# A two-layer graph network on one core: the first 32 tiles of layer one are taken from the edge list as it comes

## The chip, the core and the metric

The kernel runs on one core of one Trainium2 chip. The metric is the device time of one execution in microseconds (us), lower is better. The core has a matrix engine (PE, whose weight loads are listed as PEld), a vector engine (DVE), an activation engine (ACT), a general engine (POOL, also called GpSimd), which here issues the indirect DMAs, and a sync engine (SP), which issues most other DMAs. All DMAs run on 16 shared DMA engines.

## The reference

There are 12,500 nodes with 64 features and 212,500 edges: 200,000 drawn ones and one loop per node. The edges are sorted by target `dst`, and the loop of a node comes last among its edges.

```
h = max(layernorm(x), 0)
x = x + L0(h, weight, src, dst, etypes)
h = max(layernorm(x), 0)
x = x + L1(h, (src, dst), edge_attr, W1, b1, W2, b2)

L0: for r in range(16):
        msg += (feat[src] * (etypes == r)) @ weight[r]
    out = segment_sum(msg, dst)
L1: h = relu(concat(x[src], x[dst], edge_attr) @ W1 + b1)
    out = segment_sum(h @ W2 + b2, dst)
```

## The kernel before

**Tiles and groups.** Edges are worked off in tiles of 128, and tiles in groups of G = 4. Layer one leaves the loops out of its tiles (their part is put into the sums by `begin` and `some`, lines 724 to 763), so the edge list is first closed up: `compact` (line 427) takes one of eight parts of rows, moves the remaining edges together on DVE, and `store` (line 474) writes them to `edges_c` in memory by two indirect DMAs on POOL. `load_tiles` (line 547) loads them back as tiles (`t_in`, `t_row`), and `codes` (line 558) works out for each tile the source indices `src_c`, a code per edge (relation and place within the tile's window of WT = 12 targets) and the window's place in the running table. This makes 1563 closed-up tiles in 391 groups. The list UPTO says which tiles belong to which part; part 0 has 188.

**The front.** `load_front` (line 250) loads all of x by SP, `front` (line 265) normalizes it in nine chunks on DVE and ACT, and SP stores each chunk to `h_rows` in memory. `compact` and `codes` of part 0 run between the chunks. The first gather of layer one reads `h_rows`, so it comes after the last store. POOL meanwhile does memsets and iotas and loads the weights (lines 349 to 377: `none`, `wrel` twice, `first_row`, `place_row`, `w1ab` twice, `b1_bc`, `w2b` twice, `zero`), eleven DMAs.

**Layer one** is the loop at lines 867 to 919. In turn `it` it gathers group `it`: `gather` (line 618) issues four indirect DMAs on POOL, each of which brings 128 rows of 256 bytes into a `rows` buffer; there are 14 of these (pool `land`). `relations` (line 631) makes one-hot rows `oh_r` of relation and place on ACT, four `Abs` (`off_r`) and one `Relu` per group, with four buffers. `products` (line 845) multiplies on PE, and `add` (line 855) adds the product to the table on DVE at a place read from a row of places. The first products wait for turn BEGIN + 1 = 9, and the adds for turn 10, since the table has to be begun by then, which needs the loops of the first nodes (`loops`, line 490, on DVE, stored to `t_loop` by POOL in turns 3 and 4). From there two groups are worked off per turn until the lag is gone; `turns` (line 106) makes these orders. Each of the 47 long steps FIN1 ends a pair of node blocks: `finish` (line 657) multiplies the table by `wrel` (`pT`), adds to x, normalizes, and stores `a_rows` and `b_rows`.

**Work beside it.** `beside_part(c)` (line 816) is a generator that is advanced by one step with each add. It prepares part c + 1 (`load_rows`, `compact`, `load_tiles`, `codes`), loads further loops and so on. What is left of it is done where the next part begins.

**Layer two** (line 947) gathers `a_rows` in 416 groups in the same manner. SP loads a window of `b_rows` for each group into one of NBW = 10 buffers `b_win`.

**Order.** Instructions issued through the wrappers `V_, S_, T_, Q_, P_` (class `InOrder`, lines 301 to 315) keep the order of the program on DVE, ACT, PE, SP and POOL; all others are placed by a scheduler that knows only estimated durations. Most of layers one and two goes through the wrappers, and the profile gives these instructions the wrapper's line, L310. Each engine runs its queue in order and waits at an instruction whose data is not there.

**Bounds.** Where the fixed windows of a program step hold the edges is decided by the data, so `bounds` (line 133) lists limits on `dst` at some edges; if one fails, `flag` is set and a general program, `in_any_order`, runs behind.

The order of the start is this:

```
h_of = front(fr, xf)
for _ in range(2):
    next(h_of)
for _ in compact(0, rows_0, V, lambda n: ()):
    pass
q, row = load_tiles(0, nc.sync)
for _ in range(3):
    next(h_of)
for _ in codes(0, q, row, psA, V, S, T, lambda n: ()):
    pass
loops_0 = load_loops(0)
```

Of the kernel before, what the change touches and what calls it, by code (L numbers as in the profile page):

```python
# [45 lines left out]
P = 128  # L48
# [35 lines left out]
CL = 202  # L84
PARTS = EP // (P * ROW)
UPTO = [0, 188, 384, 580, 776, 972, 1168, 1364, 2 * -(-NTC // 2)]
PMAX = max(b - a for a, b in zip(UPTO, UPTO[1:]))
# [17 lines left out]

def turns(lag, n, early=lambda g: 0):

    most, least = lag
    of = {}
    for g in range(n):  # L110
        of.setdefault(max(early(g), g + max(least, min(most, most - (g - (n - 40)) // 4))), []).append(g)
    return of
# [15 lines left out]

FIN1 = [8 * (k + 1) + SLACK - 1 for k in range(NREG)] + [384, 388, NGC - 1]
STEP1 = [sum(f < g for f in FIN1) for g in range(NGC)]  # L130


def bounds():

    least, most = [(0, 0)], [(0, 0)]
    for k in range(NFIN - 1):
        b0, nb = BLOCKS[k]
        end = (b0 + nb) * P

        x = (FIN1[k] + 1) * G * P  # L140
        least.append((x + end, end))
        ahead = end + AHEAD - WT
        if x + ahead < E:
            most.append((x + ahead, ahead))
        x = (FIN[k] + 1) * G * P
        least.append((x, end))
        most.append((min(x, E) - 1, end + AHEAD2 - W))
    for c in range(1, PARTS):
        most.append((c * P * ROW, c * P * ROW - UPTO[c] * P))
    for q in range(1, LPARTS):  # L150
        least.append((q * P * LROW, LOOPS_UPTO[q]))
    return least, most
# [3 lines left out]
WE = W + EA  # L156
NBW = 10
RG = 8
# [21 lines left out]
def gnn_kernel(  # L180
    ctx: ExitStack, tc, x, src, dst, etype, attr, src_t, dst_t, attr_t, rows_c, rows_l, first, last, step_t, step_c, least, most, w_rel, w1, b1, w2, b2, out
):
# [33 lines left out]

    NCK = 3 * PARTS + 4 * LPARTS + 3
    odds = keep.tile([P, NCK], F32, name="odds")
# [66 lines left out]
    def in_order():  # L285
        with ExitStack() as c2:
# [42 lines left out]
            c4 = c3.enter_context(ExitStack())  # L329
            fr = c4.enter_context(tc.tile_pool(name="front", bufs=2))  # L330
            rows_0 = load_rows(0, nc.sync)
            xf = load_front(fr)
# [15 lines left out]
            G_.memset(none, -1.0)  # L348
            G_.dma_start(t_loop[N:, :].rearrange("n o -> o n"), none)
            wrel = own.tile([P, RH, D], F32, name="wrel")  # L350
            for k in range(2):
                G_.dma_start(wrel[k * D : (k + 1) * D], w_rel[k::2].rearrange("r i o -> i r o"))
# [3 lines left out]
            G_.dma_start(first_row, first.unsqueeze(0))  # L356
# [3 lines left out]
            G_.dma_start(place_row, step_t[::G].unsqueeze(0))  # L360
            w1ab = own.tile([P, 2, D], F32, name="w1ab")
            for k in range(2):
                G_.dma_start(w1ab[k * D : (k + 1) * D], w1[: 2 * D].rearrange("(k i) o -> i k o", k=2))
            b1_bc = own.tile([P, D], F32, name="b1_bc")
            G_.dma_start(b1_bc, b1.unsqueeze(0).to_broadcast([P, D]))
            w2b = own.tile([DA, D], F32, name="w2b")
            G_.dma_start(w2b[:D, :], w2)
            G_.dma_start(w2b[D:DA, :], b2.unsqueeze(0))

# [6 lines left out]
            G_.memset(zero, 0.0)  # L376
            G_.dma_start(b_rows[NB * P :, :], zero)

# [95 lines left out]
            def store(table, to, rows, rest, pause=16):  # L474

                for half in range(2):
# [6 lines left out]
                    yield from rest(pause)  # L483

            def load_loops(q):
# [72 lines left out]
            def codes(c, q, row, psA, V, S, T, rest):  # L558
# [9 lines left out]
                codes_of[c] = code, places  # L568
                word, first_d = q[:n, :, :, 0], q[:n, :, 0, 1]
                low, rel, even = (i_[:n, k] for k in range(3))  # L570
                sf, d, ok = (f[:n, k] for k in range(3))
# [225 lines left out]
            def chain(*parts):  # L797
                for part in parts:
                    yield from part
# [27 lines left out]

            def first_layer(psA, loops_0):
# [6 lines left out]
                n_of, oh_of, rows_of, pa_of = {}, {}, {}, {}  # L835
                of_pe = turns(L1_PE, NGC, lambda g: BEGIN + 1 + g // 2)
                of_add = turns(L1_ADD, NGC, lambda g: BEGIN + 2 + g // 2)
                of_oh = turns((0, 0), NGC, lambda g: BEGIN + g // 2 if g < 2 * BEGIN else 0)

                def part_of(g):  # L840

                    c = sum(g * G >= b for b in UPTO[1:])
                    return c, g * G - UPTO[c]

# [10 lines left out]
                def add(a, i):  # L855
                    k = a * G + i
                    if i < n_of[a]:
                        ca, ka = part_of(a)
                        ka += i
                        if ka % RG == 0:  # L860
                            n = min(RG, UPTO[ca + 1] - UPTO[ca] - ka)
                            at.update(enumerate(windows(codes_of[ca][1], ka, SN + AHEAD - WT, V_, n), k))
                        to = tables[STEP1[a] % 2][:, :, bass.ds(at.pop(k), WT)]
                        V_.tensor_tensor(to, to, pa_of[a][:, i, :].rearrange("p (r n) -> p r n", r=RH), op=ALU.add)

                at = {}
                for it in range(NGC + L1_ADD[1]):
                    g = it
                    if g < NGC:
                        c, kc = part_of(g)  # L870
                        if kc == 0:
# [3 lines left out]
                        if g % 56 == 16 and g // 56 < NB // LB:  # L875
                            load_x(g // 56 * LB, Q_)
                        rows_of[g], n_of[g] = gather(h_rows[:, :], src_c, g, NTC)
                    for g in of_oh.get(it, []):
                        c, kc = part_of(g)
                        oh_of[g] = relations(codes_of[c][0], kc, n_of[g])  # L880
                    if it < BEGIN:
                        for _ in range(G):
                            next(first_loops, None)
                        if it == BEGIN - 2:
                            for _ in first_loops:
                                pass
# [628 lines left out]
```

## Time and profile before

| what | us |
|---|---|
| median of 3 runs (lowest to highest) | 4140.85 (4140.67 to 4142.58) |
| the profiled execution | 4139.85 |
| its span in the profile | 4137.5 |
| POOL busy | 3083.6 |
| PE busy / weight loads | 2619.0 / 2087.4 |
| ACT busy | 1609.3 |
| DVE busy | 1136.7 |
| first gather of `h_rows` starts | 50.19 |
| POOL waits between the layers, once | 17.2 |

Spans and medians are of single executions; busy times are sums over one engine's instructions. A line of a timeline gives the start, the duration, the engine, the line, the operation, output and input, the count, and in brackets how long the engine was idle before and what ended it. An engine name with a q (SPq) is the queue that issues DMAs; its time is that of issuing, not of the transfer. In a row of windows each engine has its busy time and its number of instructions; then come the clock granted to PE (1.00 is full), the busy share of the 16 DMA engines and the GB/s moved.

PE's granted clock is 1.00 for the first 75 us and 0.50 from 125 us on.

### The profile page before, as it was taken

Reading aid. Unit: us, or ns where it says so; the run is one execution under the profiler, and the core shown is the slowest. Engines: PE = TensorE matmul, PEld = TensorE weight load, DVE = VectorE, ACT = ScalarE, POOL = GpSimd, SP = SyncE. Lnnn points to the kernel's source line nnn. Section 1 sums busy time; section 2 is a strip of 40 time slices with the busy share of each in tenths; the row PEclk is TensorE's granted clock in tenths of the full one; section 3 lists DMA queues with packets and bytes.
Section 4 is the critical chain, followed back from the end, with each engine's and each line's share of the span. In section 5 each row is a group of like instructions: output and inputs, shape, how many; then the busy total and the mean of one; then the engine's idle time right before and its main releaser. Section 6 shows DMA issues by size and latency. Waiting matters only on the chain. (4 is left out here: it accounts for less than half of the span.)

```text
span 4137.5 us, 50346 instructions
## 1 busy us (share of the span) xinstructions
PE 2619.0 (63%) x15332; PEld 2087.4 (50%) x15332; DVE 1136.7 (27%) x4570; ACT 1609.3 (39%) x3131; POOL 3083.6 (75%) x3279
## 2 busy tenths in 40 slices
PE   1676666667676767666666666665666666666655
PEld 0444444444444444444555555555555555555555
DVE  6343334333343333323211111111111111111111
ACT  5545454444444444544422322322322223223222
POOL 5777777777777777777677777777777777777776
PEclk9555555555555555555555555555555555555555
DMA  4212222112212121111111211212121221112111
GB/s 111 47 38 53 47 43 49 41 37 44 43 42 45 37 45 38 38 38 37 39 42 40 44 41 40 45 40 44 41 42 42 43 42 42 42 41 44 42 39 34
DMA packets 217607, 180.05 MB, mean 44 GB/s; under 512 B 147587, under 2 KB 156198, under 8 KB 216390
## 3 DMA queue, kind: packets, MB, share of 16 engines
q0 software_dynamic: 104576, 107.96, 14.2%
q1 hardware_dynamic: 99453, 65.57, 5.9%
q10 hardware_dynamic: 13298, 3.20, 0.3%
q8 instruction: 125, 2.05, 0.2%
q14 instruction: 155, 1.27, 0.1%
HBM read 161.49 MB, written 14.99 MB: 43 GB/s over the span
## 5 line engine op out<-in xcount | busy, mean ns | idle before, releaser
L310 POOL DMA_INDIRECT rows<-a_rows,src_i x1661 | 1567.1, 943 | 523.3 <-issue 426.2
L310 POOL DMA_INDIRECT rows<-h_rows,src_c x1563 | 1483.4, 949 | 503.7 <-issue 390.7
L310 PE MATMUL pz<-b_win,of_edges 48*128 48x64 f32 x3322 | 815.4, 424 | 712.7 <-ACT of_edges L310 708.4
L310 PE MATMUL pa<-oh_r,rows 128*64 128x96 f32 x6252 | 856.9, 387 | 621.4 <-DMA rows<-h_rows,src_c 552.3
L310 PEld LDWEIGHTS pz<-b_win,of_edges 48*128 48x128 f32 x3322 | 738.5, 325 | 760.8 <-ACT of_edges L310 739.7
L310 PEld LDWEIGHTS pa<-oh_r,rows 128*64 128x64 f32 x6252 | 471.1, 207 | 941.1 <-DMA rows<-h_rows,src_c 615.9
L310 ACT ACTIVATE hid<-z 128x256 f32<-128x256 f32 x416 | 173.1, 416 | 1449.7 <-DVE z L310 1399.2
L310 DVE TENSOR_TENSOR z<-pz,rows 128x256 f32<-128x256 f32 x416 | 176.5, 424 | 1692.9 <-DMA rows<-a_rows,src_i 1539.9
L310 ACT ACTIVATE off_r<-iota_s,code 128x192 bf16<-128x192 f32 x1563 | 578.6, 442 | 1.9 <-issue 1.9
L310 PE MATMUL pa<-oh,hid 128*65 128x40 f32 x3322 | 456.7, 312 | 39.8 <-ACT hid L310 26.9
L310 DVE TENSOR_TENSOR table<-table,pa 128x96 f32 x1563 | 395.5, 253 | 301.6 <-PE pa L310 194.3
L310 ACT ACTIVATE oh_r<-off_r 128x768 f32<-128x768 bf16 x391 | 329.3, 842 | 302.2 <-PE pa L310 292.6
L310 PEld LDWEIGHTS pa<-oh,hid 128*65 128x65 f32 x3322 | 395.9, 226 | 90.0 <-ACT hid L310 30.9
L310 PE MATMUL pT<-wrel,table 128*128 128x64 f32 x1568 | 432.5, 434 | 0.0
L310 PEld LDWEIGHTS pT<-wrel,table 128*128 128x128 f32 x1568 | 362.8, 324 | 82.8 <-issue 82.5
L310 ACT ACTIVATE off<-local_bc,neg_w 40x1024 bf16<-40x1024 bf16 x208 | 235.8, 1134 | 15.6 <-DVE sums L310 8.3
L310 ACT ACTIVATE of_edges<-off 40x1024 f32<-40x1024 bf16 x208 | 219.7, 1056 | 6.6
L310 DVE SCALAR_TENSOR_TENSOR table<-b_rel,rsel,hT 128x256 f32<-128x256 f32 (+1 forms) x400 | 172.4, 472 | 96.3 <-PE hT L310 73.0
L310 DVE TENSOR_TENSOR ab<-pab,b_bc 128x64 f32<-128x64 f32 x98 | 17.6, 220 | 432.3 <-ACT ab L310 432.3
L310 DVE TENSOR_TENSOR oh<-local,iota_p 128x160 f32<-128x160 f32 x416 | 128.8, 310 | 0.0
L310 DVE TENSOR_TENSOR x_sb<-x_sb,pT 128x128 f32<-128x128 f32 (+1 forms) x50 | 14.2, 285 | 397.3 <-PE pT L310 397.3
L310 ACT ACTIVATE s_rs<-s_mv,eps 128x2 f32<-128x2 f32 (+1 forms) x50 | 14.8, 296 | 242.2 <-DVE s_mv L310 238.0
(163 smaller groups left out, 840.7 us busy)
## 6 DMA issues: line engine op xcount, KB each, us to landing
rows<-a_rows,src_i POOLq DMA_INDIRECT x1661, 2.5
rows<-h_rows,src_c POOLq DMA_INDIRECT x1563, 2.4
local_bc<-dst_l SPq DMA_DIRECT2D x104, 160.0 KB
of_edges<-in_attr_t SPq DMA_DIRECT2D x104, 64.0 KB
b_win<-b_rows SPq DMA_DIRECT2D x416, 10.0 KB
b_rel<-t_loop SPq DMA_DIRECT2D x48, 128.0 KB
l_in<-in_rows_l SPq DMA_DIRECT2D x4, 1009.5 KB
b_h<-h_rows SPq DMA_DIRECT2D x48, 64.0 KB
```

The source lines that it names most:

```text
L310: last_ins[self.engine] = getattr(self.engine, name)(*args, **kw)
```

## The change

The first eight groups of layer one (RAWG = 8, 32 tiles, 4096 edges) are taken from the edge list as it stands, with the loops in it, and the first 28 closed-up tiles (CUT = 28) are left out. For the 32 raw tiles POOL gathers rows of `x` itself, not of `h_rows`, while the front runs; the gathered rows are normalized afterwards, in place (`rows_raw`). Loops and edges of no relation get a code that matches nothing (`codes_raw`). Closed-up tiles 28 to 30 or so hold edges that are among the 4096 too; `codes` of part 0 masks those by their place in the list (`place_w`). 

The group numbers of layer one shift by SHIFT = 8 - 28/4 = 1, so there are 392 groups, of which 384 are gathered within the loop, and the loop's turn `it` gathers group it + 8. At turn BEGIN = 8, when products begin, 16 groups are waiting where 8 were.

The eleven weight DMAs move from POOL's start into a generator `weights` on SP's ordered queue, as the first steps of `beside_part(0)`. The number of `b_win` buffers goes from 10 to 8. Two limits on `dst` are added to the bounds.

```
+RAWG = 8
+RAWT = RAWG * G
+RAWE = RAWT * P
+CUT = 28
+SHIFT = RAWG - CUT // G
+NG1 = NGC + SHIFT
...
+    most.append((RAWE, RAWE - CUT * P))
+    most.append((RAWE - 1, SN + AHEAD - WT))
...
-NBW = 10
+NBW = 8
...
+            raw = own.tile([P, 4, RAWT], I32, name="raw")
+            nc.sync.dma_start(raw, raw_c)
+            raw_rows = [own.tile([P, 2, G, D], F32, name=f"raw_rows{k}") for k in range(RAWG // 2)]
+            raw_tiles = iter(range(RAWT))
+            def gather_raw(n):
+                for _, k in zip(range(n), raw_tiles):
+                    g, i = divmod(k, G)
+                    P_.indirect_dma_start(
+                        out=raw_rows[g // 2][:, g % 2, i, :],
+                        out_offset=None,
+                        in_=x[:, :],
+                        in_offset=bass.IndirectOffsetOnAxis(ap=raw[:, 3, k : k + 1], axis=0),
+                    )
+                return ()
             rows_0 = load_rows(0, nc.sync)
...
-            G_.dma_start(t_loop[N:, :].rearrange("n o -> o n"), none)
...
+            def weights():
+                for k in range(2):
+                    Q_.dma_start(wrel[k * D : (k + 1) * D], w_rel[k::2].rearrange("r i o -> i r o"))
+                    Q_.dma_start(w1ab[k * D : (k + 1) * D], w1[: 2 * D].rearrange("(k i) o -> i k o", k=2))
+                    yield
...
+            def codes_raw():
...
+                Q_.dma_start(f, raw_f.unsqueeze(0).to_broadcast([P, RAWT]))
+                Q_.dma_start(row, raw_f.unsqueeze(0))
...
+            def rows_raw(k):
+                n = 2 * G
+                r = raw_rows[k].rearrange("p a g d -> p (a g) d")
...
+                for i in range(n):
+                    V_.bn_stats(st[:, i, :], r[:, i, :])
+                for i in range(n):
+                    V_.bn_aggr(mv[:, i, :], st[:, i, :])
+                S_.activation(rs[:, 0, :], mv[:, :, 1], AF.Sqrt, bias=eps, scale=1.0)
+                yield
+                V_.reciprocal(rs[:, 1, :], rs[:, 0, :])
+                V_.scalar_tensor_tensor(rs[:, 2, :], mv[:, :, 0], -1.0, rs[:, 1, :], op0=ALU.mult, op1=ALU.mult)
+                for i in range(n):
+                    S_.activation(r[:, i, :], r[:, i, :], AF.Relu, bias=rs[:, 2, i : i + 1], scale=rs[:, 1, i : i + 1])
+                yield
...
+                if c == 0:
+                    place_w = prep.tile([PMAX // 2, 2, P], F32, name="t_place", bufs=1)[:n]
+                    G_.iota(place_w, pattern=[[P, 2], [1, P]], base=0, channel_multiplier=2 * P, allow_small_or_imprecise_dtypes=True)
+                    V.tensor_tensor(place_w, place_w, q[:n, :, :, 1], op=ALU.add)
...
+                if c == 0:
+                    V.scalar_tensor_tensor(ok, place_w, float(RAWE), ok, op0=ALU.is_ge, op1=ALU.mult)
...
             def beside_part(c, psA):
+                if c == 0:
+                    yield from weights()
...
+                more = chain(codes_raw(), *(rows_raw(k) for k in range(RAWG // 2)))
...
-                for it in range(NGC + L1_ADD[1]):
-                    g = it
-                    if g < NGC:
+                for it in range(NG1 - RAWG + L1_ADD[1]):
+                    g = it + RAWG
+                    if g < NG1:
...
                     if it < BEGIN:
                         for _ in range(G):
                             next(first_loops, None)
+                        for _ in range(2):
+                            next(more, None)
...
-                for _ in compact(0, rows_0, V, lambda n: ()):
+                gather_raw(9)
+                for _ in compact(0, rows_0, V, lambda n: gather_raw(4) if n > 8 else ()):
                     pass
+                gather_raw(RAWT)
                 q, row = load_tiles(0, nc.sync)
```

The raw gathers go through the ordered wrapper of POOL: nine, then compact's first store, four, its second store, four, and the remaining fifteen.

More of the change, by code (lines that the diff above doesn't have):

```diff
@@ L103, with turns @@
 BEGIN = 8
-def turns(lag, n, early=lambda g: 0):
+def turns(lag, n, early=lambda g: 0, before=0):
     most, least = lag
@@ L110, in turns @@
     for g in range(n):
-        of.setdefault(max(early(g), g + max(least, min(most, most - (g - (n - 40)) // 4))), []).append(g)
+        of.setdefault(max(early(g), g - before + max(least, min(most, most - (g - (n - 40)) // 4))), []).append(g)
     return of
@@ L127 @@
 STEP = [sum(f < g for f in FIN) for g in range(NGR)]
-FIN1 = [8 * (k + 1) + SLACK - 1 for k in range(NREG)] + [384, 388, NGC - 1]
-STEP1 = [sum(f < g for f in FIN1) for g in range(NGC)]
+FIN1 = [8 * (k + 1) + SLACK - 1 + SHIFT for k in range(NREG)] + [384 + SHIFT, 388 + SHIFT, NG1 - 1]
+STEP1 = [sum(f < g for f in FIN1) for g in range(NG1)]
 def bounds():
@@ L138, in bounds @@
         end = (b0 + nb) * P
-        x = (FIN1[k] + 1) * G * P
+        x = (FIN1[k] + 1 - SHIFT) * G * P
         least.append((x + end, end))
@@ L180, in gnn_kernel @@
 def gnn_kernel(
-    ctx: ExitStack, tc, x, src, dst, etype, attr, src_t, dst_t, attr_t, rows_c, rows_l, first, last, step_t, step_c, least, most, w_rel, w1, b1, w2, b2, out
+    ctx: ExitStack, tc, x, src, dst, etype, attr, src_t, dst_t, attr_t, rows_c, rows_l, raw_c, raw_f, first, last, step_t, step_c, least, most, w_rel, w1, b1, w2, b2, out
 ):
@@ L215, in gnn_kernel @@
     flag = keep.tile([1, 1], I32, name="flag")
-    NCK = 3 * PARTS + 4 * LPARTS + 3
+    NCK = 3 * PARTS + 4 * LPARTS + 4
     odds = keep.tile([P, NCK], F32, name="odds")
@@ L348, in in_order @@
             G_.memset(none, -1.0)
-            G_.dma_start(t_loop[N:, :].rearrange("n o -> o n"), none)
             wrel = own.tile([P, RH, D], F32, name="wrel")
-            for k in range(2):
-                G_.dma_start(wrel[k * D : (k + 1) * D], w_rel[k::2].rearrange("r i o -> i r o"))
             local = own.tile([P, NT], F32, name="local")
@@ L355, in in_order @@
             first_row = own.tile([1, NGR], I32, name="first_row")
-            G_.dma_start(first_row, first.unsqueeze(0))
             src_i = own.tile([P, NT], I32, name="src_i")
             place_row = own.tile([1, NGR], I32, name="place_row")
-            G_.dma_start(place_row, step_t[::G].unsqueeze(0))
             w1ab = own.tile([P, 2, D], F32, name="w1ab")
-            for k in range(2):
-                G_.dma_start(w1ab[k * D : (k + 1) * D], w1[: 2 * D].rearrange("(k i) o -> i k o", k=2))
             b1_bc = own.tile([P, D], F32, name="b1_bc")
-            G_.dma_start(b1_bc, b1.unsqueeze(0).to_broadcast([P, D]))
             w2b = own.tile([DA, D], F32, name="w2b")
-            G_.dma_start(w2b[:D, :], w2)
-            G_.dma_start(w2b[D:DA, :], b2.unsqueeze(0))
             b_win = [own.tile([WE, D], F32, name=f"b_win{k}") for k in range(NBW)]
@@ L376, in in_order @@
             G_.memset(zero, 0.0)
-            G_.dma_start(b_rows[NB * P :, :], zero)
+            def weights():
[3 more added lines that the diff above has]
+                    yield
+                Q_.dma_start(b1_bc, b1.unsqueeze(0).to_broadcast([P, D]))
+                Q_.dma_start(t_loop[N:, :].rearrange("n o -> o n"), none)
+                yield
+                Q_.dma_start(first_row, first.unsqueeze(0))
+                Q_.dma_start(place_row, step_t[::G].unsqueeze(0))
+                yield
+                Q_.dma_start(w2b[:D, :], w2)
+                Q_.dma_start(w2b[D:DA, :], b2.unsqueeze(0))
+                yield
+                Q_.dma_start(b_rows[NB * P :, :], zero)
+                yield
             def rest(n):
@@ L483, in store @@
                     yield from rest(pause)
+            raw_code = own.tile([P, RAWT], F32, name="raw_code")
+            raw_places = own.tile([1, RAWT], I32, name="raw_places")
+            def codes_raw():
+                f = prep.tile([P, RAWT], I32, name="raw_f", bufs=1)
+                row = prep.tile([1, RAWT], I32, name="raw_r", bufs=1)
+                even = prep.tile([P, RAWT], I32, name="raw_e", bufs=1)
+                rel = prep.tile([P, RAWT], I32, name="raw_t", bufs=1)
+                d = prep.tile([P, RAWT], F32, name="raw_d", bufs=1)
+                ok = prep.tile([P, RAWT], F32, name="raw_ok", bufs=1)
+                bad = prep.tile([P, RAWT], F32, name="raw_bad", bufs=1)
+                Q_.dma_start(f, raw_f.unsqueeze(0).to_broadcast([P, RAWT]))
+                Q_.dma_start(row, raw_f.unsqueeze(0))
+                dst_r, next_r, typ_r = raw[:, 0], raw[:, 1], raw[:, 2]
+                V_.tensor_scalar(rel, typ_r, 1.0, 0.0, op0=ALU.add, op1=ALU.max)
+                V_.tensor_single_scalar(rel, rel, float(R + 1), op=ALU.min)
+                V_.tensor_single_scalar(even, rel, 1, op=ALU.bitwise_and)
+                yield
+                V_.tensor_tensor(ok, dst_r, next_r, op=ALU.is_equal)
+                V_.scalar_tensor_tensor(ok, rel, 1.0, ok, op0=ALU.is_ge, op1=ALU.mult)
+                V_.scalar_tensor_tensor(ok, rel, float(R), ok, op0=ALU.is_le, op1=ALU.mult)
+                yield
+                V_.tensor_tensor(d, dst_r, f, op=ALU.subtract)
+                V_.scalar_tensor_tensor(bad, d, float(WT), d, op0=ALU.is_ge, op1=ALU.mult, accum_out=next(odds_of))
+                V_.scalar_tensor_tensor(d, rel, float(WT // 2), d, op0=ALU.mult, op1=ALU.add)
+                yield
+                V_.scalar_tensor_tensor(d, even, -float(HW - WT // 2), d, op0=ALU.mult, op1=ALU.add)
+                V_.scalar_tensor_tensor(d, d, float(1 + HW - WT), ok, op0=ALU.add, op1=ALU.mult)
+                V_.tensor_scalar(raw_code, d, -1.0, 1.0, op0=ALU.mult, op1=ALU.add)
+                yield
+                V_.tensor_scalar(raw_places, row, 0.0, float(SN + AHEAD - WT), op0=ALU.max, op1=ALU.min)
+                yield
@@ new lines, in rows_raw @@
+            def rows_raw(k):
+                n = 2 * G
+                r = raw_rows[k].rearrange("p a g d -> p (a g) d")
+                st = prep.tile([P, n, 6], F32, name="raw_st")
+                mv = prep.tile([P, n, 2], F32, name="raw_mv")
+                rs = prep.tile([P, 3, n], F32, name="raw_rs")
+                for i in range(n):
[3 more added lines that the diff above has]
+                S_.activation(rs[:, 0, :], mv[:, :, 1], AF.Sqrt, bias=eps, scale=1.0)
+                yield
+                V_.reciprocal(rs[:, 1, :], rs[:, 0, :])
+                V_.scalar_tensor_tensor(rs[:, 2, :], mv[:, :, 0], -1.0, rs[:, 1, :], op0=ALU.mult, op1=ALU.mult)
+                for i in range(n):
+                    S_.activation(r[:, i, :], r[:, i, :], AF.Relu, bias=rs[:, 2, i : i + 1], scale=rs[:, 1, i : i + 1])
+                yield
@@ L835, in first_layer @@
                 n_of, oh_of, rows_of, pa_of = {}, {}, {}, {}
-                of_pe = turns(L1_PE, NGC, lambda g: BEGIN + 1 + g // 2)
-                of_add = turns(L1_ADD, NGC, lambda g: BEGIN + 2 + g // 2)
-                of_oh = turns((0, 0), NGC, lambda g: BEGIN + g // 2 if g < 2 * BEGIN else 0)
-                def part_of(g):
-                    c = sum(g * G >= b for b in UPTO[1:])
-                    return c, g * G - UPTO[c]
+                of_pe = turns(L1_PE, NG1, lambda g: BEGIN + 1 + g // 2, RAWG)
+                of_add = turns(L1_ADD, NG1, lambda g: BEGIN + 2 + g // 2, RAWG)
+                of_oh = turns((0, 0), NG1, lambda g: BEGIN + g // 2, RAWG)
+                for g in range(RAWG):
+                    rows_of[g], n_of[g] = raw_rows[g // 2][:, g % 2], G
+                more = chain(codes_raw(), *(rows_raw(k) for k in range(RAWG // 2)))
+                def part_of(g):
+                    if g < RAWG:
+                        return (raw_code, raw_places), g * G, RAWT
+                    k = (g - SHIFT) * G
+                    c = sum(k >= b for b in UPTO[1:])
+                    return codes_of[c], k - UPTO[c], UPTO[c + 1] - UPTO[c]
                 def products(g, i):
@@ L857, in add @@
                     if i < n_of[a]:
-                        ca, ka = part_of(a)
+                        of, ka, n = part_of(a)
                         ka += i
-                        if ka % RG == 0:
-                            n = min(RG, UPTO[ca + 1] - UPTO[ca] - ka)
-                            at.update(enumerate(windows(codes_of[ca][1], ka, SN + AHEAD - WT, V_, n), k))
+                        if k not in at:
+                            n = min(RG - ka % RG, n - ka)
+                            at.update(enumerate(windows(of[1], ka, SN + AHEAD - WT, V_, n), k))
                         to = tables[STEP1[a] % 2][:, :, bass.ds(at.pop(k), WT)]
@@ L866, in first_layer @@
                 at = {}
-                for it in range(NGC + L1_ADD[1]):
-                    g = it
-                    if g < NGC:
-                        c, kc = part_of(g)
-                        if kc == 0:
+                for it in range(NG1 - RAWG + L1_ADD[1]):
+                    g = it + RAWG
+                    if g < NG1:
+                        k = (g - SHIFT) * G
+                        if it == 0 or k in UPTO:
+                            c = sum(k >= b for b in UPTO[1:])
                             for _ in coming:
@@ L874, in first_layer @@
                             coming = beside_part(c, psA)
-                        if g % 56 == 16 and g // 56 < NB // LB:
-                            load_x(g // 56 * LB, Q_)
-                        rows_of[g], n_of[g] = gather(h_rows[:, :], src_c, g, NTC)
+                        if it % 56 == 4 and it // 56 < NB // LB:
+                            load_x(it // 56 * LB, Q_)
+                        rows_of[g], n_of[g] = gather(h_rows[:, :], src_c, g - SHIFT, NTC)
                     for g in of_oh.get(it, []):
-                        c, kc = part_of(g)
-                        oh_of[g] = relations(codes_of[c][0], kc, n_of[g])
+                        of, k, _ = part_of(g)
+                        oh_of[g] = relations(of[0], k, n_of[g])
                     if it < BEGIN:
@@ L883, in first_layer @@
                             next(first_loops, None)
+                        for _ in range(2):
+                            next(more, None)
                         if it == BEGIN - 2:
                             for _ in first_loops:
+                                pass
+                            for _ in more:
                                 pass
@@ L1494 @@
         "rows_l": rows(LPARTS, LROW, LWIN),
+        "raw_c": np.ascontiguousarray(
+            np.stack([by_tile(a)[:, :RAWT] for a in (dst_p[:EP], dst_p[1 : EP + 1], typ_p[:EP], src_p[:EP])], 1)
+        ),
+        "raw_f": np.ascontiguousarray(dst_p[:RAWE:P]),
         "least": limits(LEAST),
@@ L1497 @@
         "step_t": np.repeat(np.array([BLOCKS[k][0] * P for k in STEP], np.int32), G),
-        "step_c": np.repeat(np.array([BLOCKS[k][0] * P for k in STEP1], np.int32), G),
+        "step_c": np.repeat(np.array([BLOCKS[k][0] * P for k in STEP1[SHIFT:]], np.int32), G),
         "w_rel": np.ascontiguousarray(L0_gnn_weight),
```

## The prediction

> **What bounds the kernel now.** I read the page's busy times first, then the costliest groups, then POOL's own timeline. The chain of waits on the page covers only the last dozen microseconds here, so POOL's timeline does its work. POOL is busy 75% of the span, PE 63%, ACT 39%, DVE 27%, but the busy share is not what decides; the gaps between POOL's instructions are.
>
> ```profile
> POOL 5777777777777777777677777777777777777776
> ...
> L310 POOL DMA_INDIRECT rows<-a_rows,src_i x1661 | 1567.1, 943 | 523.3 <-issue 426.2
> L310 POOL DMA_INDIRECT rows<-h_rows,src_c x1563 | 1483.4, 949 | 503.7 <-issue 390.7
> ```
>
> One gather of 128 rows takes some 945 ns and is followed by 300 ns that waits for nothing but issue. Together the two groups hold 1567.1 + 523.3 + 1483.4 + 503.7 = 4077.6 us of the 4137.5 us span. From 50.19 us on POOL issues one gather every 1.249 us (five from 63.12 to 69.36 us), and the only long gaps are the one before 50.19 us and 17.2 us between the layers. So a gather taken out of this row is worth 1.249 us, and the moment the row starts is worth its own length.
>
> ```profile
> 4.72 0.93 POOL L352 DMA_DIRECT2D wrel<-in_w_rel  x1
> ...
> 11.60 0.53 POOL L367 DMA_DIRECT2D w2b<-in_w  x1 [1.72 <-DMA wrel<-in_w_rel]
> 13.31 0.50 POOL L368 DMA_DIRECT2D w2b<-in_b  x1 [1.18 <-DMA t_loop<-none]
> ...
> 16.30 0.96 POOL L310 DMA_INDIRECT edges_c<-c_out,c_to  x1 [2.13 <-DVE r_st L233]
> ...
> 21.62 0.94 POOL L310 DMA_INDIRECT edges_c<-c_out,c_to  x1 [3.77 <-DMA edges_c<-c_out,c_to]
> 50.19 1.37 POOL L310 DMA_INDIRECT rows<-h_rows,src_c  x1 [27.64 <-DVE l_f L310]
> 51.87 0.96 POOL L310 DMA_INDIRECT rows<-h_rows,src_c  x1 [0.30 <-issue]
> ```
>
> This is POOL's start: idle from 22.6 to 50.19 us. The profile puts the long wait down to DVE, but the gather reads h_rows, whose last store SP issued at 47.5 us; SP's own first read of it goes out at 49.27 us. So the front (normalizing x and storing h_rows) sets 50.19. I also see that POOL's ninth DMA waits for the landing of its first (wrel, 4.72 to 11.60) and its tenth for its second: eight are in flight at most.
>
> ```profile
> 5.36 0.15 DVE L440 CAST c_d<-c_in 128x1 f32<-128x1 int32 x1 [4.33 <-DMA c_in<-in_rows_c]
> ...
> 45.30 0.28 ACT L236 ACTIVATE r_rs<-r_mv,eps 128x4 f32<-128x4 f32 x1
> ...
> 10.00:12.50 2.50, 0.00 (x0) 0.00 (x0) 2.30 (x10) 0.00 (x0) 0.53 (x1) 1.00 1.04 260
> ...
> 20.00:25.00 5.00, 0.00 (x0) 0.00 (x0) 5.00 (x50) 4.45 (x14) 0.94 (x1) 1.00 0.46 157
> 25.00:30.00 5.00, 0.00 (x0) 0.00 (x0) 5.00 (x48) 4.48 (x15) 0.00 (x0) 1.00 0.33 114
> ```
>
> The front in timeline and windows (columns PE, PEld, DVE, ACT, POOL, clock, DMA share, GB/s): DVE is busy almost without a gap from 5.36 us, when c_in lands, to 41 us; ACT likewise from 15 to 47.5. The DMA engines are full from 2.5 to 20 us and under half used on average after that.
>
> **Step 1, what is left out.** The row after the front loses 28 gathers: 28 x 1.249 = 35.0 us. The first layer keeps 1563 - 28 = 1535 there.
>
> **Step 2, 32 raw gathers in POOL's front.** They cost nothing if they end before h_rows is there. POOL's memsets and iotas end at 4.8 us; six hid memsets and zero (0.4 together) come next, and the iota for place_w adds 0.3 (iota_s: 0.28). The index load raw is issued first; c_in took 5.36 - 1.56 = 3.8 us from issue to use, so raw is there at 4.5. Start 5.5. Then 32 x 1.25, two stores of compact at 1.25 each, and 0.4 because a first gather took 1.37: 5.5 + 40 + 2.5 + 0.4 = 48.4 us. The cover is 50.19 less 48.4, only 1.8 us, plus whatever the front itself slips.
>
> No row shows gathers beside the full DMA engines, so I bound it. Low end: no slower than 1.25. High end: wrel is 512 rows of 256 bytes, four gathers' worth, and landed in 6.9 us, 1.7 each; the 12 gathers up to 20 us then cost 12 x 0.45 = 5.4 more. I take nothing, because the eleven weight DMAs leave just this stretch, and they were some 1500 such rows, as many as 12 gathers, all landed by 17.5 us (w1ab: 9.4 us to landing): 1.05 us for a gather's worth. The second compact store waits for the first to land (16.30 + 0.96 to 21.62: 4.4 us); four gathers, 5 us, now stand between them. With a queue ahead of it that is 0 to 4 us; I take 0.
>
> **Step 3, the front itself.** SP issues raw ahead of c_in: 0.6 us (c_in's own issue is 0.57), and DVE and ACT, both full, shift by it. codes of part 0 gains place_w: one add like t_f at 33.73 (0.41) and one product like that at 35.83 (0.40), in DVE's full stretch: 0.8. The second store moves from 21.62 to about 24.7, so t_in lands some 3 us later; DVE took it 7.9 us after its issue, so I take 0, at most 3. Together +1.4: the row starts near 51.6, with 48.4 below it. Bounds: -0.4 (ACT, not DVE, holds the end, and a POOL already at work drops the extra 0.4 of a first gather) to +8 (58: all high ends of steps 2 and 3 on POOL).
>
> The Trainium skill speaks against this hiding. SBUF — State Buffer, "Who interferes with whom", says DVE instructions in a two-port mode lock GpSimd out of the port it writes descriptors through, and its measured example goes from 620 to 3100 ns. The trace's nearest row disagrees: from 50 to 60 us DVE is busy 9.09 of 10 us and the gathers take 0.94 to 0.96 us; the longest I find elsewhere is 1.55 (at 202.57). By the rule, as an estimate from that page, each gather beside DVE would take five times as long until DVE's front ends at 41 us, seven would be done by then, and the row would start near 75 us: about 4131 instead of 4107.
>
> **Step 4, the new work beside the first gathers.** Reading raw_f and codes_raw cost about 13 small DVE operations; rows_raw costs DVE 32 x (0.135 + 0.073) = 6.7 us (11 BATCH_NORM_STATS2 in 1.48, 14 AGGREGATE in 1.02) and ACT 32 x 0.34 + 4 x 0.3 = 12 us (11 ACTIVATE in 3.75). The cover: DVE waits 22.36 us before 81.86 and ACT 30.77 us before 90.67. Four rounds in turn take some 16 us, the four oh_r that fit 9 us more: ready about 36 us after the row starts, where the first products now stand 38.6 us after it. Nothing on the path.
>
> **Step 5, a backlog of 16 groups instead of 8.**
>
> ```profile
> 90.67 0.84 ACT L310 ACTIVATE oh_r<-off_r 128x768 f32<-128x768 bf16 x1 [30.77 <-PE pa L310]
> ...
> 92.93 0.84 ACT L310 ACTIVATE oh_r<-off_r 128x768 f32<-128x768 bf16 x1
> ...
> 95.19 0.84 ACT L310 ACTIVATE oh_r<-off_r 128x768 f32<-128x768 bf16 x1
> ```
>
> The groups are eaten one per 2.26 us (these rows). At PE's halved clock (0.50 from 125 us) PE is busy 33.43 of 50 us at one group per 5: 3.35. POOL has 14 land buffers, so it waits if raw's eight groups and one more are not eaten 14 groups after the row starts, 14 x 5 + 2.5 = 72.5 us on. Products start at 38.6, four groups go at once in 4, five more at 3.35 end at 59.4. Slack 13 us; cost 0. Behind a waiting gather POOL would hold t_loop's and edges_c's stores, and the loads of prepare after them.
>
> **Step 6, SP.** Eleven weight DMAs go to SP at about 0.6 each, 6.6 us, ahead of part 1's c_in. That is issued at 81.87 and used at 94.45; 12.6 less the 3.8 to landing leaves 8.8. wrel is needed by the first pT at 119.93, 30 us later. If that cover failed, DVE's adds would come a few us later, inside the 13 of step 5. b_win with 8 buffers instead of 10 still loads eight groups, 40 us, ahead. Both 0.
>
> **Sum.** -35.0 + 1.4 = -33.6. The span goes from 4137.5 to 4103.9. The profiled run took 4139.85 us, 2.35 more than its span, and the median of the runs is 1.0 above that: 4140.85 - 33.6 = 4107.3.
>
> **Rivals.**
> A: raw gathers end late and replace the front as what POOL waits for. For it: only 1.8 us of cover, full DMA engines to 20 us, the store's wait. Against: 1.05 us per gather's worth in just that stretch. POOL's row starts between 53.5 and 58: 4109 to 4114, say 4111.
> B: the catch-up stalls POOL on land for part of the gain, because rows_raw or PE is slower than I worked out: with 8 to 25 us lost, 4115 to 4132, say 4121. Against: the 13 us of slack.
> C, slower: the same place, carried through. If a group costs r us to eat, POOL stalls from 42.6 + 5r > 72.5, r = 6.0, and above 5 it loses r - 5 more on each group that follows. At r = 7 that is 5 us, then 2 for each of 16 groups: 37 us, more than the gain: 4144. The rows give 2.26 to 3.35; it would need both doubled for 80 us.
> D: the change does not do what it says, because a bound fails and the general program runs behind. In the inputs dst at edges 4095 and 4096 is 248; the new bounds are 372 and 512. With any failure the time would grow by far more than any case here. Counted with C.
>
> **How the numbers follow.** Forecast (4104.5 to 4109) 0.64, A 0.25, B 0.08, C and D 0.02, and 0.01 that it gains nothing. A measurement of this kernel can tell about 0.2%, 8 us, from no change: below 4132.5 is faster. Faster 0.96, same 0.02, slower 0.02. The range 4104.5 to 4114 holds the forecast and A, nearly 9 in 10, which its open bounds need.
>
> **What would show it.** POOL's timeline: 32 gathers from x between about 5.5 and 49 us, the first one from h_rows at 51 to 53, then 1.249 us steps without a long wait up to the 17 us between the layers; 1535 in the h_rows group. Step 2 is wrong if the gathers before 20 us stand more than 1.5 us apart, or if the last one ends after h_rows has landed; step 3 if DVE's first cast of c_in is not near 6 us; step 5 if POOL waits for PE between 100 and 200 us. The forecast is wrong if the row starts after 54.

## The result, and the profile after

| | us |
|---|---|
| before, median of 5 runs (lowest to highest) | 4140.85 (4139.63 to 4142.58) |
| after, median of 5 runs (lowest to highest) | 4120.33 (4118.31 to 4122.29) |
| ratio of the two, 95% interval | 0.995 (0.9936 to 0.9965) |
| forecast, and its range | 4107.3, 4104.5 to 4114.0 |
| profiled execution after, and its span | 4122.29, 4120.5 |

The change made the kernel faster by 20.5 us, not by the 33.6 forecast, and the time lies above the range. The direction was right; 13 us are missing.

The page of the kernel after, first the shares of POOL in 40 slices, then the costliest groups:

```profile
span 4120.5 us, 50722 instructions
...
POOL 6777777777777777777677777777777777777776
...
L321 POOL DMA_INDIRECT rows<-a_rows,src_i x1661 | 1567.2, 944 | 524.2 <-issue 441.6
L321 POOL DMA_INDIRECT rows<-h_rows,src_c x1535 | 1458.1, 950 | 485.7 <-issue 385.9
```

There are 1535 gathers of `h_rows`, 28 fewer, and each costs what it did. POOL is still the bound. So most of the missing time has to lie in when its row starts. POOL's timeline of the kernel after:

```profile
4.90 0.14 POOL L394 MEMSET zero<- 40x64 f32 x1
5.22 1.10 POOL L321 DMA_INDIRECT raw_rows<-in_x,raw  x1 [0.17 <-issue]
6.62 1.23 POOL L321 DMA_INDIRECT raw_rows<-in_x,raw  x1 [0.30 <-issue]
8.15 1.03 POOL L321 DMA_INDIRECT raw_rows<-in_x,raw  x1 [0.30 <-issue]
9.49 0.94 POOL L321 DMA_INDIRECT raw_rows<-in_x,raw  x1 [0.31 <-issue]
...
23.23 0.91 POOL L321 DMA_INDIRECT edges_c<-c_out,c_to  x1 [0.30 <-issue]
...
46.97 0.94 POOL L321 DMA_INDIRECT raw_rows<-in_x,raw  x1 [0.30 <-issue]
47.93 0.38 POOL L659 IOTA t_place<- 94x256 f32 x1
66.04 0.97 POOL L321 DMA_INDIRECT rows<-h_rows,src_c  x1 [17.73 <-DVE l_few L321]
```

The raw gathers run as worked out: first at 5.22, the last one over at 47.91, 48.4 in the forecast. But the first gather of `h_rows` starts at 66.04, not at 51.6. POOL stands idle for 17.73 us before it, and the bracket names a DVE instruction of no account (`l_few`, which only happened to end last). What really stands there is one line further up: a lone iota at 47.93, behind all the raw gathers. The timeline of all engines shows who wanted it:

```profile
5.36 0.15 DVE L474 CAST c_d<-c_in 128x1 f32<-128x1 int32 x1 [4.33 <-DMA c_in<-in_rows_c]
...
32.44 0.60 DVE L244 BATCH_NORM_STATS2 r_st<-xf 128x6 f32<-128x64 f32 x4
48.34 0.42 DVE L660 TENSOR_TENSOR t_place<-t_place,t_in 94x256 f32<-94x256 f32 x1 [15.31 <-POOL t_place L659]
...
53.72 0.32 ACT L700 COPY code<-hT 128x188 f32<-128x188 f32 x1 [15.66 <-DVE src_c L699]
...
59.02 4.42 SPq L292 DMA_DIRECT2D h_rows<-xf  x3
64.96 0.37 SPq L321 DMA_DIRECT2D b_h<-h_rows  x1
```

DVE has nothing to do from 33.03 to 48.34. It waits to add to `place_w`, in `codes` of part 0, and the rest of the front is queued behind that add: statistics of the last chunks, then ACT's passes over them, then the stores of `h_rows` at 59.02. SP's own first read of `h_rows` goes out at 64.96, 15.7 us later than before (49.27). A row of the windows, with each engine's busy time and count, then clock, DMA share and GB/s, says the same: DVE at work for 0.04 of 15 us.

```profile
33.00:48.00 15.00, 0.00 (x0) 0.00 (x0) 0.04 (x1) 5.06 (x16) 11.39 (x13) 1.00 0.43 133
```

POOL's timelines of both kernels, cut at four instants, account for all of the difference between the two profiled executions (spans 4137.5 and 4120.5):

| stretch of POOL | before | after | difference |
|---|---|---|---|
| start to first gather of `h_rows` | 50.19 | 66.04 | +15.85 |
| from there to the last gather of `h_rows` | 1985.27 | 1951.87 | -33.40 |
| from there to the first gather of `a_rows` | 18.20 | 19.17 | +0.97 |
| from there to the last gather of `a_rows` | 2072.25 | 2072.26 | 0.0 |
| from there to the end | 11.59 | 11.16 | -0.43 |
| sum | 4137.5 | 4120.5 | -17.0 |

The profiled execution of the kernel after was the slowest of its five, which is most of why it shows 17.0 and the medians 20.5. The row gave 33.4 of the 35.0 us forecast; the start took 15.85 back where 1.4 was forecast. Of the 16.6 us by which this span misses the forecast of 33.6, the start makes 14.45 and the row 1.6.

### The profile page after: what moved, and what is told of

Read it like the earlier page. It is cut to its first block, busy times and chain, and to the rows that moved or that the text cites. A ratio compares the mean times of both kernels' runs of the same rounds, so it can differ in the third digit from the quotient of the medians.

```text
span 4120.5 us, 50722 instructions
## 1 busy us (share of the span) xinstructions
PE 2601.1 (63%) x15348; PEld 2081.1 (51%) x15348; DVE 1146.8 (28%) x4662; ACT 1622.4 (39%) x3172; POOL 3082.8 (75%) x3273
## 3 DMA queue, kind: packets, MB, share of 16 engines
q1 hardware_dynamic: 101767, 66.04, 6.0%
## 5 line engine op out<-in xcount | busy, mean ns | idle before, releaser
L321 POOL DMA_INDIRECT rows<-h_rows,src_c x1535 | 1458.1, 950 | 485.7 <-issue 385.9
L321 PE MATMUL pa<-oh_r,rows 128*64 128x96 f32 x6140 | 837.5, 387 | 600.1 <-DMA rows<-h_rows,src_c 544.5
L321 PEld LDWEIGHTS pa<-oh_r,rows 128*64 128x64 f32 x6140 | 461.9, 207 | 909.5 <-DMA rows<-h_rows,src_c 601.3
L321 ACT ACTIVATE off_r<-iota_s,code 128x192 bf16<-128x192 f32 x1535 | 568.2, 442 | 0.0
```

The lines of the kernel that those rows point to most:

```text
L321: last_ins[self.engine] = getattr(self.engine, name)(*args, **kw)
```

## The experiments

Theory: the iota of `place_w` is not among POOL's first instructions, where the prediction had priced it, but behind the 32 raw gathers, and its place alone sets the late start. Times below are medians, timelines are of one execution, and each ratio is to runs of the kernel before beside that experiment (medians 4140.68 and 4141.05). Rivals: the raw gathers themselves, with two stores between them, slow POOL or the front; the mask's two DVE operations cost more than 0.8; the moved weights or the fewer `b_win` buffers cost something.

**The iota ahead of the raw gathers.** One instruction is moved, and it is issued through POOL's ordered wrapper (`P_`) instead of being placed by the scheduler (`G_`):

```
-                    place_w = prep.tile([PMAX // 2, 2, P], F32, name="t_place", bufs=1)[:n]
-                    G_.iota(place_w, pattern=[[P, 2], [1, P]], base=0, ...)
+                    place_w = place_0[:n]
...
+                place_0 = prep.tile([PMAX // 2, 2, P], F32, name="t_place", bufs=1)
+                P_.iota(place_0, pattern=[[P, 2], [1, P]], base=0, ...)
                 gather_raw(9)
```

> The changed kernel with one instruction moved: the iota that fills place_w is issued on POOL before the first raw gather instead of behind the last. Theory Q (queue): in the changed kernel the iota ran at 47.93 us, behind 32 gathers, and DVE stood 15.31 us in front of the add that reads it, with the rest of the front queued behind. Then DVE's wait vanishes and the first gather from h_rows starts at 51.0 us (50.19 of the kernel before plus 0.8 for two more DVE operations) instead of 66.04; time 4120.3 - 15.0 = 4105.3, at most 4107. Rival C (contention): the raw gathers themselves slow the front, by the DMA engines or by the port shared with DVE, and the iota only stood last in a queue that was late anyway. Then the first gather from h_rows still starts after 58 us and the time stays above 4112. Rival D (data): the second compact store and with it t_in came too late behind the gathers; then DVE waits at the next operation, which reads t_in, and the start stays above 56 us.

Measured: 4105.1 us (4104.41 to 4105.95), ratio 0.9913 (0.99 to 0.9927). Its timeline of POOL, then that of all engines:

```profile
5.00 0.36 POOL L321 IOTA t_place<- 100x256 f32 x1
...
33.42 2.28 POOL L321 DMA_INDIRECT raw_rows<-in_x,raw  x1 [0.31 <-issue]
36.00 1.42 POOL L321 DMA_INDIRECT raw_rows<-in_x,raw  x1 [0.30 <-issue]
37.73 0.95 POOL L321 DMA_INDIRECT raw_rows<-in_x,raw  x1 [0.30 <-issue]
...
49.05 1.09 POOL L321 DMA_INDIRECT raw_rows<-in_x,raw  x1 [0.30 <-issue]
50.90 0.95 POOL L321 DMA_INDIRECT rows<-h_rows,src_c  x1 [0.75 <-DVE l_few L321]
```

```profile
33.12 0.40 DVE L659 TENSOR_TENSOR t_place<-t_place,t_in 94x256 f32<-94x256 f32 x1
33.45 0.28 DVE L662 TENSOR_SCALAR t_i<-t_in 94x256 int32<-94x256 int32 x1
33.65 0.28 DVE L663 TENSOR_SCALAR t_i<-t_in 94x256 int32<-94x256 int32 x1
...
49.84 0.37 SPq L321 DMA_DIRECT2D b_h<-h_rows  x1
```

The add has no bracket: DVE does not wait any more, and the row starts at 50.90. Moving one instruction of 0.38 us brings 15.2 us back. All 32 gathers and both stores still run beside the front, so they are not what held it up. This version beats both kernels. Cut at the same instants and set against the kernel before it has +0.71, -35.65, +1.19, +0.06 and -0.51, in all -34.2.

**The last 15 raw gathers behind `codes`.** The other way round: the iota stays in `codes`, and the gathers ahead of it become fewer.

```
-                gather_raw(RAWT)
                 q, row = load_tiles(0, nc.sync)
...
+                gather_raw(RAWT)
                 loops_0 = load_loops(0)
```

> The changed kernel with the last fifteen raw gathers issued behind codes of part 0 in the program instead of before its loads, so that the iota falls behind 18 gathers and runs near 30.8 us; nothing else is touched and the iota stays where it was written. Theory Q: DVE reaches the add at about 33 us and finds place_w done, so there is no wait: first gather from h_rows near 51.0, time 4105 to 4107, as with the iota first. Rival C: the number of gathers beside the front is the same, so the start stays after 58 us. Rival D: as the loads of t_in leave as before, the start stays above 56.

Measured: 4105.29 (4104.41 to 4111.26), ratio 0.9913 (0.99 to 0.9927). POOL's timeline:

```profile
28.97 0.38 POOL L659 IOTA t_place<- 94x256 f32 x1
...
51.18 0.94 POOL L321 DMA_INDIRECT rows<-h_rows,src_c  x1 [0.76 <-DVE l_few L321]
```

Here the iota is written as in the kernel after. Two edits with only one thing in common, the iota's place against the time at which DVE needs it, give the same time.

**A half dose.** The iota stands behind 24 raw gathers (a `gather_raw(7)` ahead of it and the remaining eight behind).

```
+                gather_raw(7)
+                P_.iota(place_0, pattern=[[P, 2], [1, P]], base=0, ...)
                 gather_raw(RAWT)
```

> A dose: the iota behind 24 raw gathers. The 25th gather of the changed kernel started at 38.24 us, so the iota ends near 38.4 and DVE, ready for it at 33.0, waits 5.4 us instead of 15.3. Theory Q: first gather from h_rows at 51.0 + 5.4 = 56.4, time 4105.3 + 5.4 = 4110.7. Rivals C and D: no step that follows the iota's place; the start within 2 us of that of the other variants.

Measured: 4111.64 (4110.16 to 4114.14), ratio 0.9928 (0.9914 to 0.9941). POOL's timeline, then that of all engines:

```profile
37.94 0.38 POOL L321 IOTA t_place<- 100x256 f32 x1
38.48 1.14 POOL L321 DMA_INDIRECT raw_rows<-in_x,raw  x1 [0.16 <-issue]
...
41.17 1.63 POOL L321 DMA_INDIRECT raw_rows<-in_x,raw  x1 [0.30 <-issue]
...
56.26 0.94 POOL L321 DMA_INDIRECT rows<-h_rows,src_c  x1 [7.22 <-DVE l_few L321]
```

```profile
38.35 0.42 DVE L659 TENSOR_TENSOR t_place<-t_place,t_in 94x256 f32<-94x256 f32 x1 [5.12 <-POOL t_place L321]
```

With waits of 0, 5.12 and 15.31 us on DVE the row starts at 50.90, 56.26 and 66.04, that is 5.36 and 15.14 us later, and the medians are 4105.1, 4111.64 and 4120.33: 6.5 and 15.2 more. The wait goes into the time one for one, within 1.5 us.

**No mask.** The iota, the add and the product with `place_w` are left out, so the edges of the first 4096 that stand in tiles 28 to 30 are counted twice.

```
-                if c == 0:
-                    place_w = ...
-                    G_.iota(place_w, ...)
-                    V.tensor_tensor(place_w, place_w, q[:n, :, :, 1], op=ALU.add)
...
-                if c == 0:
-                    V.scalar_tensor_tensor(ok, place_w, float(RAWE), ok, op0=ALU.is_ge, op1=ALU.mult)
```

> The changed kernel without place_w: the iota, the add and the product that mask edges of the first 4096 in part 0 are left out, so edges in tiles 28 to 30 count twice. It prices the two DVE operations against the kernel with the iota first. Theory Q with my step 3: 0.8 us less, first gather from h_rows at 50.2, time 4104.5. If ACT alone sets the end of the front: no difference, under 0.3 us. Rivals C and D: the start stays above 56, as the gathers and stores are all there.

Measured: 4106.13 (4104.57 to 4106.83), ratio 0.9915 (0.9902 to 0.9929); the row starts at 50.66. That is no faster than with the mask and the iota ahead (4105.1, row at 50.90). The work of the mask costs nothing that shows in the time; only the iota's place did.

**The weights on SP alone**, in the kernel before:

```
-            for k in range(2):
-                G_.dma_start(wrel[k * D : (k + 1) * D], w_rel[k::2]...)
...
+            def weights():
+                for k in range(2):
+                    Q_.dma_start(wrel[k * D : (k + 1) * D], w_rel[k::2]...)
...
             def beside_part(c, psA):
+                if c == 0:
+                    yield from weights()
```

> The kernel before with one part of the change alone: the eleven weight DMAs go from POOL's start to SP's ordered queue as the first steps beside part 0. My step 6: 0, between 4139.5 and 4142, first gather from h_rows at 50.2. Rival: the weights free the full DMA engines up to 20 us, so the front ends earlier: 1 us or more gained; or they hold c_in of part 1 back and DVE with it: 1 us or more lost.

Measured: 4139.88 (4138.79 to 4146.03, 11 runs), ratio 0.9997 (0.9988 to 1.0006). The row starts at 49.74. No change that can be told.

**Eight `b_win` buffers alone**, in the kernel before:

```
-NBW = 10
+NBW = 8
```

> The kernel before with 8 buffers for b_win instead of 10 and nothing else. My step 6: 0, between 4139.5 and 4142. Rival: the windows of b_rows come late in layer two and each of the 416 groups loses something; 0.01 us a group would be 4 us.

Measured: 4140.23 (4138.58 to 4148.06, 11 runs), ratio 0.9998 (0.9989 to 1.0007). No change that can be told either.

**More of the same.** With the iota ahead, ten raw groups instead of eight and 36 tiles left out (`NHID` goes down to make room):

```
-RAWG = 8
+RAWG = 10
...
-CUT = 28
+CUT = 36
...
-            NHID = 6
+            NHID = 4
```

> The iota first, and ten raw groups (40 tiles) with 36 closed-up tiles left out instead of eight with 28; the buffers hid go from 6 to 4 to make room. With the iota first POOL stands idle for some 2 us before the front ends at 50.9. Theory: eight more raw gathers at 1.249 end POOL's front at 59.0, which is then what sets the first gather from h_rows, and eight fewer follow: 4105.1 + 8.1 - 10.0 = 4103.2. Rival: the backlog of 18 groups makes POOL wait for a land buffer between 100 and 200 us, or four hid buffers slow layer two; then 4105 or more.

Measured: 4106.13 (4105.12 to 4113.69), ratio 0.9916 (0.9902 to 0.9929): nothing gained over 4105.1. POOL's timeline:

```profile
59.29 0.95 POOL L321 DMA_INDIRECT raw_rows<-in_x,raw  x1 [0.30 <-issue]
60.54 0.94 POOL L321 DMA_INDIRECT rows<-h_rows,src_c  x1 [0.30 <-DVE raw_code L321]
```

The expectation missed. It took it that POOL still stood idle for some 2 us ahead of the first gather of `h_rows`; with eight raw groups and the iota ahead it was 0.75, since two raw gathers had run long. Eight more gathers then move the start by 60.54 - 50.90 = 9.6 us, and eight fewer behind it give back 10.0. The rival, a stall on a landing buffer, did not appear: from 60.54 us to the end of layer one POOL is never idle for more than 0.32 us at a time. Front and raw gathers are in balance at eight groups.

**Eight landing buffers instead of 14**, with the iota ahead, to see whether the prediction's account of the backlog holds:

```
-            land = c2.enter_context(tc.tile_pool(name="land", bufs=14))
+            land = c2.enter_context(tc.tile_pool(name="land", bufs=8))
```

> The iota first, with 8 land buffers instead of 14, to measure the slack of step 5. With the iota first the eight raw groups and the first group from h_rows are eaten 54.7 us after the row of gathers starts. With 8 buffers POOL needs the first of them back 8 x 5 + 2.5 = 42.5 us after that start, so if step 5 has the mechanism right it waits some 12 us there, near 93 us, once: 4105.1 + 12 = 4117, and the slack with 14 buffers is 72.5 - 54.7 = 18 us. Rival: the backlog doesn't bind at all and the time stays within 1 us of 4105; or eight buffers are too few in the steady row too and the loss is above 20.

Measured: 4117.01 (4116.36 to 4118.07), ratio 0.9943 (0.9929 to 0.9956). POOL's timeline:

```profile
105.36 1.03 POOL L321 DMA_INDIRECT rows<-h_rows,src_c  x1 [12.27 <-PE pa L321]
```

Here a stall of POOL on a buffer does appear, and it is named after PE's product, 12.27 us of it, all of which reach the end: 4117.0 - 4105.1 = 11.9. It ends 105.36 - 50.98 = 54.4 us after the start of that row. With 14 buffers the same buffer is asked for again only 14 x 5 + 2.5 = 72.5 us after it, which leaves 18 us of slack.

## Why the prediction was off

**What failed: step 2, the iota.** The prediction placed it with POOL's first instructions: "six hid memsets and zero (0.4 together) come next, and the iota for place_w adds 0.3". The six memsets and `zero` did run there, at 4.71 to 5.04. The iota did not. It is written in `codes`, which the program calls after `gather_raw(RAWT)`, and it ran behind all 32 gathers, at 47.93. Its duration (0.38, priced at 0.3) did not matter; its place cost 15.31 us of DVE's time and moved the start of the row by 15.85, where the sum allowed 1.4 and no wait of DVE for the iota. What was missed is the work queued behind a waiting instruction on DVE: the very chain, front to `h_rows` to the first gather, that the prediction had named as what sets 50.19.

It could have been read in the program and in the profile before. There POOL ran the `hid` memsets, which need nothing, right behind a DMA issue that had waited until 13.31:

```profile
13.80 0.29 POOL L374 MEMSET hid<- 128x4 f32 x6
```

In these timelines an instruction on POOL starts only behind what stands ahead of it, and every gather put into an idle stretch is a queue for whatever POOL still has to do for others. The 28 us in which POOL was idle were not idle for the iota.

None of the rivals named this. A looked for POOL being late; POOL was on time, and DVE was late because of it. The text did name the sign by which to see that the forecast had failed, though not the cause: "wrong if the row starts after 54".

**What held.** With that one instruction moved, the kernel takes 4105.1, inside the forecast's own 4104.5 to 4109.

- Step 1: 35.0 us for 28 gathers. The row lost 35.65 with the iota ahead (the first gather's extra 0.42 among it) and 33.40 in the kernel after. Of the 2.25 us between these, 1.9 are in the gathers' busy time (1458.1 against 1456.2 for 1535); why they ran longer is open.
- Step 2, gathers beside full DMA engines: from 2.5 to 20 us their share is 0.93, the first three steps are 1.40, 1.53 and 1.34 us, and from 9.49 on about 1.25. The high end of 5.4 us did not occur. The second store came at 23.23 and waited for nothing.
- Step 3: the two operations of the mask, 0.8 forecast, showed no cost in the time (the row starts 0.24 later with them), and neither did the index load issued ahead of `c_in` (0.6 forecast: `c_d` is cast at 5.36 in both kernels). With the iota ahead the row starts 0.7 later than before where 1.4 were forecast.
- Step 4: 16 us for the four rounds of `rows_raw`. They run from 75.53 to 91.0.

ACT's timeline of the kernel after, from there on, shows the raw groups being made ready:

```profile
92.42 0.84 ACT L321 ACTIVATE oh_r<-off_r 128x768 f32<-128x768 bf16 x1
...
94.67 0.84 ACT L321 ACTIVATE oh_r<-off_r 128x768 f32<-128x768 bf16 x1
...
106.53 0.84 ACT L321 ACTIVATE oh_r<-off_r 128x768 f32<-128x768 bf16 x1 [5.13 <-PE pa L321]
```

- Step 5: the groups are made one per 2.25 us, four fit, and the fifth waits until PE starts on them. In the kernel after no step of POOL in which PE is named is longer than the usual 0.3 us, so there is no stall. The mechanism is real, as eight buffers show, and 14 were enough by 18 us where 13 were forecast. So B and C did not happen, for the reason given.
- Step 6: 0, and alone each of the two edits measured 0 within 0.12%.

## What to carry to other kernels

When an idle engine is given new work, list what else stands in its queue for others, and find where each such instruction is written, not where one would put it: anything small that another engine waits for goes ahead of the new work. In the profile such a fault shows as a short instruction at the end of a long row of one engine and a long bracket on another engine just after it; the wait that the bound itself shows may name something quite different. When the filling work ends just as the old wait ends, stop: more of it only moves the start.

## What was not expected of the hardware

Some raw gathers ran long beside one block of DVE's work. In the kernel with the iota ahead the two at 33.42 and 36.00 took 2.28 and 1.42 us where 0.94 is usual, while DVE ran the 94x256 operations of `codes` (33.12 to 37.5, the first of them shown above). With ten raw groups they took 2.27 and 1.42, at 33.49 and 36.07; with the last 15 gathers behind `codes` 2.51 and 1.42, at 33.47 and 36.29. With the half dose `codes` ran from 38.35 on, and the long ones moved along: 1.14 at 38.48 and 1.63 at 41.17. In the kernel after, where no gather ran beside that block, no raw gather took more than 1.23. Without the mask, where the block lacks two operations and starts at 33.16, only one ran long: 2.16 at 33.23, and 1.08 at 35.70. With the iota ahead the two cost POOL some 1.8 us. POOL was done at 50.14, and the row started at 50.90; so it was luck that this cost, which the prediction put at nothing, did not reach the time.

The Trainium skill, SBUF — State Buffer, "Who interferes with whom", says that DVE instructions in a two-port mode keep GpSimd from the port pair they share, and lists `tensor_scalar` among those that can enter such a mode. The direction agrees here; its estimate in the prediction, five times as long for every gather beside DVE, does not: the other 30 gathers took 0.94 to 1.1 us, most of them with DVE at work, and the sum was 1.8 us, not 24. (The example of 620 and 3100 ns, from which that estimate was made, stands on the same page under "A bandwidth-pool intuition that's wrong".) The prediction's own reading, that gathers are as fast beside a busy DVE, holds for the statistics of the front and not for this block; and in the window from 50 to 60 us that it quoted for 0.94 to 0.96, the first gather, at 50.19, took 1.37. Which of the block's instructions does it, and through what, is not shown; only that the long gathers go where the block goes.
